# Layer 0 attention emitted by a phase in a group's period, and layer 1's row transforms stored frequency by frequency

## The chip, the core and the metric

The kernel runs on one core of one Trainium2 chip. The core has a matrix engine (TensorE, called PE in the profile; its weight loads are listed apart as PEld), a vector engine (VectorE, DVE), a scalar engine (ScalarE, ACT), a general engine (GpSimd, POOL) and SyncE (SP), which here only issues transfers. Each engine works through its own queue strictly in order; an instruction at the head of a queue waits until what it reads is written and what it overwrites has been read. Data lies in SBUF (128 partitions) and in PSUM, the accumulators into which PE writes.

The metric is the device time of one execution in microseconds. The kernel before takes 3742.2 us, the median of three runs (3740.39 to 3743.42). The profile comes from a further execution of the same program.

## The reference

The input `x` has 4 batches of 32 time steps, each 128 nodes by 128 features, in fp32 (8 MB). It goes through three layers in two sublayers each. The change touches layer 0 and the start of layer 1; the rest is an attention with a linear kernel and an expert network (layer 2), and a linear attention and a recurrent network (layer 3). Cut to what matters here:

```python
# layer 0:  x = x + conv_attn_hybrid(group_norm(x, 32 groups))
def gat(h, adj):                    # 128 images of 128 nodes x 128 features, 4 heads of 32
    q, k, v = heads(h @ Wq), heads(h @ Wk), heads(h @ Wv)
    scores = einsum('bnhd,bmhd->bhnm', q, k) / sqrt(32)
    scores = where(adj == 0, -1e9, scores)
    return h + softmax(scores) @ v @ Wo + bo
def mamba(xt):                      # every node a sequence of 32 steps, 256 channels, 16 states
    xc, z = split(xt @ in_proj); xc = silu(conv4(xc) + conv_b)
    dbc = xc @ x_proj               # 8 numbers for dt, B (16), C (16)
    dt = softplus(dbc[..., :8] @ dt_w + dt_b)
    h_t = exp(dt_t * A) * h_{t-1} + (dt_t * xc_t) * B_t        # the scan
    y_t = sum_s(h_t * C_t) + Dp * xc_t
    return (y * silu(z)) @ out_w + out_b
h  = layernorm(h + gat(h))          # per image
xt = layernorm(xt + mamba(xt))      # per node, after a transposition

# layer 1:  every 128 x 128 image is a token: instance norm, spectral convolutions for
#           keys, queries, values (rfft2, 16 x 9 modes), attention over 32 tokens, two mixers
x_ft = rfftn(instance_norm(tokens)) # the rows' transform: 65 numbers (cos, sin) of 128 columns
```

## The kernel before, in words

**Layer 0** runs batch by batch (four batches, b0 to b3), and each batch has two stages: the attention (`gat`) and the scan (`mamba`). All of `x` lies in SBUF in the tile `X`.

*The attention stage* treats a batch as eight groups of four time steps, so a tile is 128 x 512. For one group, in the order of the data: PE transposes the four images of `X` (kind `x`), DVE normalises them (`hg`, L454), PE forms q and k (`q`, L458), ACT copies them out (`qo`, L461), PE forms the values (`v`, L467) and DVE copies them (`vo`, L470). PE writes the scores of the four heads with the mask added (`sc`, L538 and L546). For each head DVE takes the row minima (`smin`, L555; the scores carry a minus sign), ACT exponentiates (`expo`, four instructions each, L560), DVE sums and inverts (`den`, L567 and L568), POOL scales (`scale`, L572). For each of the four images PE transposes the scaled weights (`turn`, L273), DVE or ACT copies them (`eT`, L580) and PE multiplies by the values (`att`, L587). ACT fetches the attention output (`o`, L594), PE projects it (`proj`, L600), DVE adds the residual (`r`, L604), which POOL made before (`base`, L531), and takes the statistics (`stats`, L609, L611); POOL raises the variance to the power -1/2 (`power`, L615 to L618), ACT normalises (`norm`, L623), PE transposes back and ACT stores the result to `h1` (`store`, L632).

Four more pieces of work lie in the same stage. (1) The end of the batch before, its output's normalisation (kinds `csums`, `cstats`, `cpower`, `cnorm`, L966 to L1010). (2) The group-norm statistics of the next batch (`gat_head`, one kind `head`): eight transposes of `X` each followed by a DVE statistic (L368), then DVE L377, PE L382, DVE L386 to L389, PE L382, DVE L392, and POOL's power L395. (3) The opening of the next batch (`gat_open`, kind `diag`): DVE L411 to L416, which read what L395 wrote, PE L420 and ACT L424. (4) The preparation of the first four scan steps (`mamba_block`): the convolution on PE (`conv`, eight products of 0.87 us, L1105), SiLU on ACT (L1112), the product for dt, B and C (L1117) and its copy `dbc` (L1121), the dt projection (L1128), and then softplus as a chain: ACT `abs` (L1136), ACT `exp` (L1139), DVE `relu` (L1144), ACT `one` (L1150), ACT `ln` (L1153), ACT `back` (L1156), POOL `dplus` (L1159), POOL `dsub` (L1162); last DVE `umul` (L1173), which the first states of the scan read. ACT holds one function table at a time; a change between SiLU, exp and ln is an instruction of 1.28 us in the trace.

*The scan stage* takes 32 steps of 16 states. In each step, four times: POOL multiplies dt by A (the decay, L822, tile `e` with three buffers), ACT exponentiates (L828), DVE multiplies by the state (L842) and adds the input (L850, four instructions, or one, L862, with the inputs made on ACT, L858); PE reads the state out (L880) with diagonal matrices that ACT (L834) and POOL (L839, tile `Dp`) make. The first step's states are made on ACT without a decay (L852).

*What sets the order.* Each stage is written as parts: (engine, estimated cost, function, predecessors, buffers taken and freed). `Parts.emit` sorts them into one sequence. With `by_rank` it takes, again and again, the part of lowest rank among those whose predecessors and buffers have been emitted; `mamba` uses it already, the rank being step group x period + a phase per kind. Without it, it plans: it keeps an estimated clock per engine, looks at the first `window` parts, takes the earliest start and within `patience` of it the lowest rank, and counts 1.3 us for a change of ACT's table. `gat` uses the planner, with a rank of `at * 144.5 + GAT_RANKS[kind]` and `PREP_RANKS` for the preparation. `in_order` then fixes this sequence as each engine's queue. So the ranks decide what stands ahead of what on PE, DVE, ACT and POOL; SP's queue and the DMAs have no part in it, since a batch's `X` is loaded once at the start (the loads of batches 1 to 3 are issued then too).

**Layer 1** opens with `images`. PE transforms the rows of each image by the matrix `fr` (`rows`, L1442), four images a round, 32 rounds; ACT copies the 4 x 65 results into `Fr` (`rows_out`, L1445) and squares the image (L1449), DVE sums the squares (`groups`, L1453), PE sums those over the rows (`total`, L1457). Products without use (`stir`, L1437) stand between them. `Fr` is a view [128, image t, frequency k] of a flat tile. Then come the norm's statistics (from the frequency 0, L1483), a scaling of `Fr` in eight pieces on DVE (L1540), POOL's rewrite of frequency 0 (L1549, L1550), the products `pr` of `Fr` with `rw` (L1565 to L1567) with ACT's copies (L1568), and the column transforms `px` (L1581 to L1588): here `Fr` for one frequency, 128 rows x 128 images, is the stationary operand of PE, 32 such products and four idle ones, ended by DVE's copies (L1590). 32 products `pG` of a copy `Rb` with itself follow (L1597).

## Time and profile before

| What | Value |
|---|---|
| Median of three runs | 3742.2 us (3740.39 to 3743.42) |
| Profiled execution, its own time | 3746.08 us |
| Its span in the profile | 3744.2 us |
| Mean granted PE clock | 0.90 |
| Busy share PE, DVE, ACT, POOL | 85%, 77%, 70%, 66% |
| First row minimum to last attention output, b0 to b3 | 36.6 to 147.7, 588.9 to 695.5, 1134.8 to 1244.4, 1684.0 to 1792.7 us |
| First scan decay to last, b0 to b3 | 158.7 to 571.8, 707.1 to 1118.6, 1254.5 to 1667.5, 1802.7 to 2211.5 us |
| `px` products of layer 1 | 2309.3 to 2325.6 us |
| `pG` products of layer 1 | 2325.6 to 2334.3 us |

The profile is of one execution of 3746.08 us; its span, from the first instruction to the last, is 3744.2 us. Times of single instructions are microseconds from the span's start. The busy shares are means over the whole program; the stages have different limits, so a stage is read from its own stretch. In the slices of the page each digit is the busy share of a fortieth of the span (93.6 us) in tenths, and the line PEclk is the clock that PE was granted in tenths of full speed. A group's line gives engine, operation, output and input with shapes, the number, the busy time and the mean of one, and after the bar the time its engine had been idle before these instructions, with what ended most of it.

### The profile page before, as it was taken

To read this page: it belongs to the slowest core of one execution; us is meant where nothing else is said; L and a number is where in the kernel's file an instruction comes from. 1 tells how busy PE (TensorE), PEld (TensorE's weight loads), DVE (VectorE), ACT (ScalarE), POOL (GpSimd) and SP (SyncE) were. 2 spreads that over 40 slices of the span, in tenths; PEclk is the share of its full clock that TensorE was granted. 3 is DMA by queue.
4 is the path that set the end of the run, shared out by engine and by line. 5 is a ranking of instruction groups with operands and counts; after the bars stand their busy time and mean duration, and the time that the engine had idled before them with its cause. 6 is when DMAs were issued, how large, how long until landed. Compare 5 with 4: busy or idle time off the path is not lost.

```text
span 3744.2 us, 64945 instructions
## 1 busy us (share of the span) xinstructions
PE 3178.7 (85%) x23839; PEld 2061.9 (55%) x23839; DVE 2888.3 (77%) x6980; ACT 2619.5 (70%) x5560; POOL 2454.3 (66%) x1985
## 2 busy tenths in 40 slices
PE   7799988799888799988799988788868977898878
PEld 4455555455555455555455557555547744587655
DVE  6699997699997799987699975778869756386942
ACT  5788886798886898877889863344556664175753
POOL 3689996699996699986799960333456432076940
PEclk8899989899999899989899988888769998998999
DMA  3000000000000000000000000000020001600003
GB/s 129 1 1 1 1 1 1 1 1 1 1 1 1 1 1 1 1 1 1 1 1 1 1 20 1 1 1 1 1 91 10 1 1 47 231 1 1 1 1 91
DMA packets 51656, 61.41 MB, mean 16 GB/s; under 512 B 5850, under 2 KB 31140, under 8 KB 51204
## 3 DMA queue, kind: packets, MB, share of 16 engines
q1 hardware_dynamic: 36740, 42.12, 3.3%
q10 hardware_dynamic: 14592, 15.08, 1.2%
q8 instruction: 190, 3.11, 0.3%
q14 instruction: 134, 1.10, 0.1%
HBM read 48.80 MB, written 8.39 MB: 15 GB/s over the span
## 4 chain that ended last, share of the span: by engine, by line
PE 19%; DVE 19%; ACT 6%; POOL 3%; issue 3%; DMA 2%; SPq 0%; DVEq 0%; ACTq 0%; POOLq 0%
DVE S L850 3%; DVE pa L842 3%; PE pc L1905 2%; PE pc L1868 1%; PE pb L1883 1%; PE pt L273 1%; PE pr L3242 1%; PE pr L3235 1%; DMA w<-in_L_ffn_weight_dram 1%; PE kv L2946 1%; DVE xn L2303 1%; DVE S L862 1%; DVE t L2160 1%; PE pc L3085 1%; PE pc L1922 1%
## 5 line engine op out<-in xcount | busy, mean ns | idle before, releaser
L822 POOL TENSOR_TENSOR e<-dt,Ar 128x1024 f32<-128x1024 f32 x496 | 1190.3, 2429 | 38.4 <-ACT pa L828 36.2
L842 DVE TENSOR_TENSOR pa<-pa,S 128x1024 f32<-128x1024 f32 x496 | 608.3, 1226 | 100.9 <-ACT pa L828 100.0
L850 DVE SCALAR_TENSOR_TENSOR S<-u,BC,pa 128x256 f32<-128x256 f32 x1488 | 611.7, 476 | 22.8 <-PE yp L880 10.8
L828 ACT ACTIVATE pa<-e 128x1024 f32<-128x1024 f32 x496 | 505.2, 1019 | 135.2 <-POOL e L822 73.9
L880 PE MATMUL yp<-S,Dp 64*64 64x256 f32 x4096 | 344.5, 475 | 2.6 <-ACT S L852 1.6
L880 PE MATMUL yp<-S,D 64*64 64x256 f32 x4096 | 300.5, 407 | 42.7 <-DVE S L850 19.5
L880 PEld LDWEIGHTS yp<-S,D 64*64 64x64 f32 x4096 | 178.3, 145 | 172.4 <-DVE S L850 48.4
L834 ACT ACTIVATE D<-I,BC 128x64 f32<-128x64 f32 x1024 | 263.4, 336 | 0.1
L880 PEld LDWEIGHTS yp<-S,Dp 64*64 64x64 f32 x4096 | 169.5, 163 | 157.0 <-issue 68.6
L1105 PE MATMUL pm<-h,Wm 128*128 128x512 f32 x512 | 255.2, 620 | 0.0
L572 POOL TENSOR_TENSOR e<-e,den 128x512 f32<-128x512 f32 x128 | 131.4, 1039 | 122.2 <-DVE den L568 69.9
L858 ACT ACTIVATE ub<-u,BC 128x256 f32<-128x256 f32 x496 | 210.3, 495 | 0.3 <-DVE S L862 0.3
L898 PE MATMUL pm<-I,y 128*128 128x64 f32 x1024 | 150.3, 270 | 39.9 <-ACT y L888 39.9
L560 ACT ACTIVATE e<-sc,mn 128x128 f32<-128x128 f32 x512 | 145.2, 396 | 30.8 <-DVE mn L555 24.3
L898 PEld LDWEIGHTS pm<-I,y 128*128 128x128 f32 x1024 | 137.2, 194 | 49.1 <-ACT y L888 48.6
L839 POOL TENSOR_TENSOR Dp<-I,BC 128x256 f32<-128x256 f32 x256 | 157.2, 629 | 7.3 <-issue 7.3
L862 DVE TENSOR_TENSOR S<-pa,ub 128x1024 f32<-128x1024 f32 x124 | 151.1, 1219 | 4.1 <-ACT ub L858 0.2
L1105 PEld LDWEIGHTS pm<-h,Wm 128*128 128x128 f32 x512 | 88.0, 192 | 97.8 <-issue 80.7
L869 PE MATMUL yp<-Wm,ident 128*128 128x256 f32 x256 | 100.1, 478 | 48.8 <-ACT y L888 37.8
L555 DVE TENSOR_REDUCE mn<-sc 128x4 f32<-128x512 f32 x128 | 83.1, 681 | 58.7 <-PE sc L546 41.3
L893 PE MATMUL pm<-xc,DD 128*128 128x128 f32 x512 | 115.5, 307 | 4.4 <-DVE v L470 2.8
L1159 POOL TENSOR_TENSOR dt<-dt,u 128x1024 f32<-128x1024 f32 x32 | 75.5, 2360 | 59.0 <-ACT u L1153 59.0
(612 smaller groups left out, 8074.0 us busy)
## 6 DMA issues: line engine op xcount, KB each, us to landing
w<-in_L_ffn_weight_dram SPq DMA_DIRECT2D x22, 1024.0 KB, 14.9
w<-in_L_ffn_weight_dram ACTq DMA_DIRECT2D x10, 1024.0 KB, 14.2
out_dram<-o ACTq DMA_DIRECT2D x16, 256.0 KB, 2.9
out_dram<-o SPq DMA_DIRECT2D x16, 256.0 KB, 2.9
X<-in_x_dram SPq DMA_DIRECT2D x4, 512.0 KB, 4.8
A<-in_L_conv_A_log_dram SPq DMA_DIRECT2D x1, 2048.0 KB
cw<-in_L_conv_conv_w_dram SPq DMA_DIRECT2D x1, 512.0 KB
sh<-in_sh_dram SPq DMA_DIRECT2D x1, 512.0 KB
```

Of the source, the lines that this page charges most:

```text
L560: nc.scalar.activation(e[:, i, :], v["sc", h // 2][:, h % 2, i * P : (i + 1) * P], AF.Exp, scale=-1.0, bias=v["mn"][:, 4 * h + i : 4 * h + ...
L822: nc.gpsimd.tensor_tensor(v["e", q], node("dt").unsqueeze(1).to_broadcast([P, 4, 256]), Ar[:, 4 * q : 4 * q + 4, :], ALU.mult)
L828: nc.scalar.activation(v["a", q], v.pop(("e", q)), AF.Exp, scale=-1.0)
L834: nc.scalar.activation(v["D", q][:, r, :], I2, AF.Copy, scale=g["BC"][:, i, s : s + 1])
L839: nc.gpsimd.tensor_tensor(v["D", q], I2.unsqueeze(1).to_broadcast([P, 4, 64]), C, ALU.mult)
L842: nc.vector.tensor_tensor(v["a", q], v["a", q], S[:, 4 * q : 4 * q + 4, :], ALU.mult)
L850: nc.vector.scalar_tensor_tensor(S[:, s, :], node("u"), Bt, a[:, r, :], ALU.mult, ALU.add)
L858: nc.scalar.activation(v["b", q][:, r, :], node("u"), AF.Copy, scale=g["BC"][:, i, s : s + 1])
L862: nc.vector.tensor_tensor(S4, v.pop(("a", q)), v.pop(("b", q)), ALU.add)
L880: nc.tensor.matmul(v["y"][o : o + 64, n, :256], D[ns, r, :], S[ns, s, :], start=(s < 2), stop=(s >= 14), skip_group_check=True,)
L898: nc.tensor.matmul(v["p"][:, o : o + 64], v["y"][:, n, j * P : (j + 1) * P], I2, start=False, stop=(n == 1))
L1105: nc.tensor.matmul(g["x", j], Wm[:, q, j * P : (j + 1) * P], rows(4 * k + 3 - q), start=(q == 0), stop=(q == 3))
```

## The change

In layer 0, `gat` no longer plans. It sets `by_rank`, and a part's rank is the group's number times `GAT_PERIOD` plus a phase from `GAT_PHASES`, one per instance of a kind within a group (four for the four heads, 22 for the next batch's statistics). The closing parts of the batch before, the next batch's statistics and the preparation of the scan get phases of the same scale (kinds beginning with `c`, `head`, kinds beginning with `p`). The parts themselves, their predecessors and their buffers stay. The costs of the parts and `STRETCH` are edited beside them (one example is shown); the planner alone reads them, and this stage no longer uses it.

In layer 1, `Fr` becomes a view [128, frequency k, image t]: the rows' copies write transposed, the scaling, POOL's rewrite and the `pr` products take the other order, ACT's copies of `pr` run straight, and the stationary operand of a `px` product is 128 numbers side by side in place of 128 numbers 65 apart. In round 2 ten products without use of 512 columns stand ahead of `total`, where four stood behind it.

```diff
@@ -328,27 +328,68 @@
         return Wq, Wk, Wv, Wo, g4, far, identb, bo, nsg, nsb
 
 
-    GAT_RANKS = dict(
-        att=-3667.5, back=260, base=-11401, cnorm=19461, cpower=16969.5, cstats=-14046, csums=-2469,
-        den=-4706.5, diag=13731, eT=-6150, expo=17585, head=3158.5, hg=1067, norm=13992.5, o=-3580,
-        power=1837.5, proj=-256, q=-975, qo=-11362.5, r=1709, sc=-2224.5, scale=15762.5, smin=2891, stats=3672,
-        store=-1872.5, turn=-8022.5, v=16866, vo=-13144.5, x=-1207.5,
+    GAT_PERIOD = 13.873
+
+    GAT_PHASES = dict(
+        att=(43.17, 47.23, 51.52, 55.84),
+        back=(91.39,),
+        base=(44.71, 45.1),
+        cnorm=(-152.35,),
+        cpower=(-179.88,),
+        cstats=(-110.36,),
+        csums=(-439.61, -162.69, 141.8),
+        den=(-154.28, 33.13, -147.2, 38.09),
+        diag=(0, 0, 0, 0,
...
+        eT=(42.85, 45.28, 49.62, -132.38),
+        expo=(-129.7, 30.87, 35.85, 34.64),
+        head=(-86.83, -15.71, 29.14, -112.82, 29.32, -151.41, 45, -219.78, 126.27, -346.88, 153.77, 103.91,
+            163.07, 199.51, 173.07, 393.09, 178.51, -114.71, 218.17, 164.3, 226.97, 211.01),
+        hg=(11.65,),
+        norm=(65.37,),
+        o=(56.82,),
+        pback=(173.32,),
+        pbc=(-101.27,),
+        pbct=(160.53,),
+        pconv=(135.08, 135.08, -135.33, 6.91, 139.7, 143.45, 182.88, 251.31),
+        pdabs=(114.96, 160.52),
+        pdbc=(263.56,),
+        pdexp=(168.41, 373.45),
+        pdln=(159.59,),
+        pdplus=(172.32,),
+        pdsub=(208.08,),
+        pdtproj=(113.5, -52.72),
+        pone=(-22.14,),
+        power=(60.13,),
+        prelu=(172.01, 380.2),
+        proj=(56.9,),
+        pumul=(412.11, 456.88),
+        pxproj=(148.65,),
+        pxsilu=(-288.93, 144.55),
+        pxturn=(606.06, 420.33),
+        q=(-174.72, 14.25),
+        qo=(14.55, 16.05),
+        r=(-123.4,),
+        sc=(23.77,),
+        scale=(40.38, -149.71, -146.96, 41.09),
+        smin=(25.93, -154.82, -154.42, -156.43),
+        stats=(58.04,),
+        store=(92.77,),
+        turn=(42.58, -136.88, 48.51, -129.57),
+        v=(32.79,),
+        vo=(38.07,),
+        x=(9.51,),
     )
 
-    PREP_RANKS = dict(
-        back=6847, bc=-3164.5, bct=4342.5, conv=1651, dabs=-4328, dbc=-1187, dexp=3646.5, dln=5483,
-        dplus=-11118, dsub=-22178, dtproj=1225.5, one=6330, relu=-4091.5, umul=-8012, xproj=2450, xsilu=3831,
-        xturn=-11453,
-    )
-
     def gat_head(self, plan, b, gw, c, pm, after=()):
 
         nc, X, PE, DVE, ACT, POOL = self.nc, self.X, "PE", "DVE", "ACT", "POOL"
-        g4, hold, v, last = gw[4], plan.hold, {}, []
+        g4, hold, v, last, seen = gw[4], plan.hold, {}, [], {}
         d = [None]
 
         def add(*args):
-            plan.rank = self.GAT_RANKS["head"]
+            n = seen["head"] = seen.get("head", -1) + 1
+            plan.rank = self.GAT_PHASES["head"][n]
             return plan.add(*args)
 
         def bank():
     def gat(self, b, early, h1, S, d, gw, mw, w, m, w2, ew, ps, po, px, pm):
-        plan = Parts(latency=0.25, window=250, patience=0.15, stretch=Parts.STRETCH)
-        hold, pace = plan.hold, 144.5
-
-        def add(kind, at, *args, **kwargs):
-            plan.rank = at * pace + self.GAT_RANKS[kind]
+        plan, seen = Parts(), {}
+        plan.by_rank, hold = True, plan.hold
+
+        def add(kind, g, *args, **kwargs):
+            n = seen[kind, g] = seen.get((kind, g), -1) + 1
+            plan.rank = g * self.GAT_PERIOD + self.GAT_PHASES[kind][n]
             return plan.add(*args, **kwargs)
 
...
-            s.pop("close")(lambda kind, at, *args, **kwargs: add("c" + kind, 0, *args, **kwargs))
+            s.pop("close")(lambda kind, k, *args, **kwargs: add("c" + kind, 0, *args, **kwargs))
...
-                mins.append(add("smin", g + i / 8, DVE, 0.62, lambda i=i: smin(i), [sc, *mins], () if i else [h["mn"]]))
+                mins.append(add("smin", g, DVE, 0.6, lambda i=i: smin(i), [sc, *mins], () if i else [h["mn"]]))
...
-        def prepare(kind, at, *args, **kwargs):
-            plan.rank = self.PREP_RANKS[kind]
-            return plan.add(*args, **kwargs)
+        def prepare(kind, k, *args, **kwargs):
+            return add("p" + kind, 0, *args, **kwargs)
 
...
@@ -1415,7 +1456,7 @@
...
         flat = XG.rearrange("p a b -> p (a b)")
-        Fr = flat[:, : BT * 65].rearrange("p (t k) -> p t k", k=65)
+        Fr = flat[:, : BT * 65].rearrange("p (k t) -> p k t", k=65)
...
@@ -1442,7 +1483,7 @@
                     nc.tensor.matmul(p[:, i, :], X[:, 4 * u + i, :], self.fr, start=True, stop=True)
 
             def rows_out(u):
-                nc.scalar.copy(Fr[:, unit(u), :], S[u].pop("p"))
+                nc.scalar.copy(Fr[:, :, unit(u)], S[u].pop("p").rearrange("p t k -> p k t"))
 
...
@@ -1460,10 +1501,10 @@
                 for r in range(U + 2):
                     run(rows, r)
                     stir(128)
+                    if r == 2:
+                        for _ in range(10):
+                            stir(512)
                     run(total, r - 2)
-                    if r == 2:
-                        for _ in range(4):
-                            stir(512)
...
@@ -1476,7 +1517,7 @@
 
 
         with self.pool("l1ps", 2, True) as ps:
-            F0 = Fr[:, :, 0].rearrange("p (b t) -> p b t", b=B)
+            F0 = Fr[:, 0, :].rearrange("p (b t) -> p b t", b=B)
...
@@ -1538,16 +1579,16 @@
             for q in range(8):
                 ts = slice(16 * q, 16 * q + 16)
                 nc.vector.scalar_tensor_tensor(
-                    Fr[:, ts, 1:],
-                    Fr[:, ts, 1:],
+                    Fr[:, 1:, ts],
+                    Fr[:, 1:, ts],
                     rs[:, 0, q // 2 : q // 2 + 1],
-                    sr[:, 0, ts].unsqueeze(2).to_broadcast([P, 16, 64]),
+                    sr[:, 0, ts].unsqueeze(1).to_broadcast([P, 64, 16]),
                     ALU.mult,
                     ALU.mult,
                 )
                 if q == 0:
                     nc.gpsimd.tensor_tensor(vf, vf, sr[:, 0, :], ALU.mult)
-                    nc.gpsimd.tensor_tensor(Fr[:, :, 0], vf, sr[:, 1, :], ALU.add)
+                    nc.gpsimd.tensor_tensor(Fr[:, 0, :], vf, sr[:, 1, :], ALU.add)
 
...
@@ -1561,11 +1602,11 @@
             Rb = flat[:, BT * 65 : BT * 65 + 32 * P].rearrange("p (k t) -> p k t", t=P)
             for q in range(8):
                 ts = slice(16 * q, 16 * q + 16)
-                p = pr.tile([P, 16, 32], F32, tag="pr", name="pr")
-                nc.tensor.matmul(p[:64], rw[:, :64], Fr[:, ts, 0:32], start=True, stop=True)
-                nc.tensor.matmul(p[64:], rw[:, :64], Fr[:, ts, 32:64], start=True, stop=False)
-                nc.tensor.matmul(p[64:, :, 0], rw[:, 64:], Fr[:, ts, 64], start=False, stop=True)
-                nc.scalar.copy(Rb[:, :, ts], p.rearrange("p t k -> p k t"))
+                p = pr.tile([P, 32, 16], F32, tag="pr", name="pr")
+                nc.tensor.matmul(p[:64], rw[:, :64], Fr[:, 0:32, ts], start=True, stop=True)
+                nc.tensor.matmul(p[64:], rw[:, :64], Fr[:, 32:64, ts], start=True, stop=False)
+                nc.tensor.matmul(p[64:, 0, :], rw[:, 64:], Fr[:, 64, ts], start=False, stop=True)
+                nc.scalar.copy(Rb[:, :, ts], p)
...
@@ -1578,14 +1619,14 @@
                 lo = p[:, 2 if k in (0, 15, 16) else (k - 1) // 7, : 14 * 34].rearrange("p (n c) -> p n c", c=34)
                 if k in (0, 16):
                     o = lo[:, 3 if k == 0 else 1, :]
-                    nc.tensor.matmul(o, Fr[:, :, k], fw[:, 0, :], start=True, stop=k == 0)
+                    nc.tensor.matmul(o, Fr[:, k, :], fw[:, 0, :], start=True, stop=k == 0)
                     if k:
-                        nc.tensor.matmul(o, Fr[:, :, 32 + k], fw[:, 2, :], start=False, stop=True)
+                        nc.tensor.matmul(o, Fr[:, 32 + k, :], fw[:, 2, :], start=False, stop=True)
                     continue
                 j = (k - 1) % 7
                 o = lo[:, 0:3:2, :] if k == 15 else lo[:, j : 14 - j : 13 - 2 * j, :]
-                nc.tensor.matmul(o, Fr[:, :, k], fw[:, 0:1, :].to_broadcast([P, 2, 34]), start=True, stop=False)
-                nc.tensor.matmul(o, Fr[:, :, 32 + k], fw[:, 1:3, :], start=False, stop=True)
+                nc.tensor.matmul(o, Fr[:, k, :], fw[:, 0:1, :].to_broadcast([P, 2, 34]), start=True, stop=False)
+                nc.tensor.matmul(o, Fr[:, 32 + k, :], fw[:, 1:3, :], start=False, stop=True)
```

## The prediction

> **What bounds the kernel now.** The change touches two places, so I read the page for their share, then each stretch on its own. First the page: the span, and the slices of PE, DVE, ACT and POOL with PE's granted clock.
>
> ```profile
> span 3744.2 us, 64945 instructions
> PE   7799988799888799988799988788868977898878
> DVE  6699997699997799987699975778869756386942
> ACT  5788886798886898877889863344556664175753
> POOL 3689996699996699986799960333456432076940
> PEclk8899989899999899989899988888769998998999
> ```
>
> The span repeats one pattern four times up to slice 24: an attention stage of about 1.4 slices in which DVE and POOL drop to 6 or 7, then a scan at 9. That is layer 0, a batch at a time. Its attention stages, from first row minimum to last attention output, are the next view: busy time of PE, PEld, DVE, ACT, POOL, then granted clock, of batches 1, 0, 2, 3.
>
> ```profile
> 588.90:695.50 106.60, 90.55 (x852) 55.51 (x850) 77.76 (x194) 81.16 (x213) 64.93 (x80) 0.98 0.01 1
> 36.60:147.70 111.10, 94.96 (x858) 58.14 (x859) 79.10 (x194) 80.17 (x210) 59.66 (x73) 0.94 0.04 16
> 1134.80:1244.40 109.60, 93.86 (x857) 57.34 (x856) 78.53 (x195) 81.41 (x213) 65.03 (x80) 0.95 0.01 1
> 1684.00:1792.70 108.70, 90.34 (x842) 54.72 (x840) 76.32 (x191) 81.29 (x213) 65.00 (x80) 0.95 0.00 1
> ```
>
> No engine is full: PE 85%, the others 60 to 76%. The stage is bound by chains between the engines' queues, which is what an order can change. DVE's groups over batch 1's stage (number | busy, mean ns | idle before):
>
> ```profile
> L567 DVE TENSOR_REDUCE den<-e 128x4 f32<-128x512 f32 x32 | 21.6, 674 | 1.7 <-ACT e L560 1.2
> L555 DVE TENSOR_REDUCE mn<-sc 128x4 f32<-128x512 f32 x32 | 20.8, 680 | 11.2 <-PE sc L546 8.8 <-ACT e L560 2.4
> L580 DVE COPY eT<-pm 128x512 f32<-128x512 f32 x16 | 10.9, 679 | 5.7 <-PE pm L273 5.7
> ```
>
> The second place is layer 1's row transforms. In order of time (start, us, what), with a pair of each kind of weight load and two lines for a clash of DVE with POOL that I need below:
>
> ```profile
> 712.33 2.39 POOL L822 TENSOR_TENSOR e<-dt,Ar 128x1024 f32<-128x1024 f32 x1
> 712.43 2.31 DVE L411 TENSOR_TENSOR gc<-gd 128x1 f32<-128x1 f32 x1 [6.22 <-POOL gd L395]
> ...
> 2310.36 0.56 PEld L1587 LDWEIGHTS px<-fw,XG 128*128 128x128 f32 x2
> 2310.82 0.56 PEld L1588 LDWEIGHTS px<-fw,XG 128*128 128x128 f32 x2
> ...
> 2325.63 8.71 PEld L1597 LDWEIGHTS pG<-XG 128*128 128x128 f32 x64
> 2325.97 1.61 DVE L1590 COPY Xm<-px 128x238 f32<-128x238 f32 x6 [20.14 <-PE px L1583]
> ...
> 2583.65 5.47 POOL L2080 TENSOR_TENSOR X<-X,t 128x256 f32<-128x256 f32 x8
> 2583.68 5.52 DVE L1982 TENSOR_TENSOR dg<-n,ident 16x64 f32<-16x64 f32 x1
> ```
>
> The px products step by 0.46 us a pair at full clock, their weights being a column of `Fr` at a stride of 65 numbers; the pG products, whose weights lie side by side, step by 0.22 once the clock is full. DVE waits 20.1 us for px: PE alone sets this stretch.
>
> **Layer 1, part by part.** *Weights in line.* From 2309.26 to 2325.63 (16.4 us) PE does 32 px pairs and 4 filler pairs. At 0.235 a pair (between pG's 0.22 and the row transforms' 0.97 us for four pairs) that is 36 x 0.235 = 8.5: -7.9. Ends: 0 if the stride isn't the reason; -0.9 if the clock stands at half throughout (pairs of in-line weights step by 0.43 at 2284 to 2286, half clock). I take -7.9, since pG is the nearest row. *pG after it* starts at half clock (until 2328.8) and takes 8.7; 32 pairs at 0.22 are 7.1: -1.5, or 0. *Gaps in POOL's write*: L1550 writes `Fr`'s first frequency with a stride in 1.32 us, its twin L1549 in line in 0.45; PE waits for it at 2297.6, so -0.8. *Ten idle products ahead of `total`, for four behind it.* PE waits 4.1 us for `sg` from 2228.4; the ten fill that. A product costs 0.86 at full clock (two of the 0.43 us instructions of L1437): 8.6 us to 2237.0 against 2237.8 before, -0.8. If the half-clock step of 2229.8 to 2236.6 still comes they end at 2240.4, +2.6; all at half +7.7. Between these I take 0. *Copies that now transpose* (L1445, runs of four numbers, PSUM read at a stride): L1264 writes such runs and reads PSUM at a stride, 578 ns for 512, as a straight copy of 512 takes; so 357 stays 357, and up to 0.35 more a copy is covered by ACT's wait for DVE in each 1.34 us round (16.8 us in 32). Upper end +0.1 a round, +3. *Scaling L1540* in runs of 16: 1.27 each, 0, upper end +2; the rw products likewise 0. Sum: -7.9 - 1.5 - 0.8 = -10.
>
> A rule of the Trainium skill (SBUF — State Buffer, "Door 1: The DMA port swizzle") speaks both ways here: SBUF serves 16-byte lines, so strided fp32 reads pay, while any PSUM access out of line slows matmuls. The first half agrees with 0.46 against 0.22. The second says nothing of ACT's reads; the L1264 row shows none slowed.
>
> **Layer 0, the steady groups.** The order of the built program now repeats one pattern on each engine. A group's DVE work is 4 x 0.65 (mn) + 4 x (0.674 + 0.178) (den) + 2 x 0.68 (eT) + 0.68 (r) + 0.86 + 0.36 (statistics) + 0.80 (hg) + 0.68 (v) = 10.75 us. Following PE, ACT and POOL along it by the rows' durations, only `eT` after the fourth product waits, by about 0.15: 10.9 a group. Before, groups stand 8.9, 9.4, 11.3, 11.5, 15.0, 12.3 and 10.8 apart (batch 1), 79.3 in all, 83.7, 82.2 and 81.4 in batches 0, 2, 3. After: 9.6 for the first (the last block's normalisation now precedes the first exponentials, which start 3.0 us later: power 1.8 and norm 1.65 less the overlap), 5 x 10.9, and 10.1 without hg: 74.2. Savings 9.5, 5.1, 8.0, 7.2. Bounds for a step: 10.75, and the 11.4 of the least disturbed steps before. Lost at the start: 0.8 in batches 1 and 2 (one head statistic ahead of the first minimum), 2.2 in batch 0, where PE's first instruction reads batch 1's x, which lands at 30.6 us.
>
> *Last minimum to last attention output.* 27.3 before. PE has eight convolution products (0.87 each) in one run there instead of spread, but no dt projection: by the rows 24.5 (23.5 in batch 3, no head). -2.8 x 3 - 3.8. So the last output `o` comes 10.1, 7.1, 10.0 and 11.0 us earlier: 38.
>
> *From there to the scan.* The whole dt chain now stands behind `o` on ACT: dbc and the first dt product until 2.1, abs 0.55, table 1.28, exp 0.55, abs 0.5, exp 0.55, one 1.1, table 1.28, ln 1.05, so 9.0; store, norm, back to 12.3. On POOL dplus 9.1 to 11.4, three Dp (they wait for norm) to 13.1, dsub to 15.5. Before, dsub ended 4.4 us after `o`, since this chain ran under the last group. Then DVE: umul, which the scan's first states S need, is now queued behind L411 to L416, which wait for POOL's power L395, itself behind dsub, and for L387 to L389, which meet dplus, Dp and dsub on POOL and run only at 15.5: power ends at 17.5. Three decays (7.1 together, as at 1802.7) follow without a gap. L411 starts under them; in L1982's row DVE sat through eight POOL instructions in a row, so I let it wait to 24.6; umul 26.0; eight S, D, four S, table and one exp on ACT 8.5; first update L850 at 35.7. Before it stands at +26.5, +26.5, +25.6 and +20.6. In batch 3, without head, it is +30.7. Loss 9.2 + 9.2 + 10.1 + 10.1 = 38.6. Lower end: L411 passes at once (as its 159 ns in batch 0's start), 7 less a batch; upper: nothing further.
>
> By the Trainium skill (SBUF — State Buffer, "SBUF: two separate sides") the loser of the shared DVE and POOL port blocks for the other's whole instruction. Read so, L411 waits for one decay, 2.4, and the sum would be 4.7 x 3 = 14 lower. The row of L1982 (5.52 us under eight) says the whole run; it decides.
>
> So layer 0 is -38 + 38.6, about -1 with the table loads left out (8 fewer in the order, 1.28 each, on ACT where it waits anyway). Scan and later stages keep their order.
>
> **Sum**: -10 - 1 = -11, from the profiled execution's 3746.1 to 3735; that execution lies 3.9 above the median of 3742.2, so 3731. Runs differ by 0.1%; under 0.2% (7.5 us) I call no change.
>
> **Rivals.**
> - *The scan isn't held.* L411 slips in after the first decay (7.1 less 2.4 a batch, 14 over three), or the steps reach the floor 10.75: -14 and -3 more, 3714. For: POOL's `e` tile has three buffers, so its run ends; against: L1982's row.
> - *The clock turns it (slower).* With normalisation ahead of the exponentials PE has some 9 us with 3 us of work at each stage's start. In layer 1 a gap of 4.1 us stands beside a 6.8 us step at half clock (0.67 in that 10 us). One such step in the first groups costs PE 3.4 us of work, two 6.8; PE leads every group's chain. At 5 a batch: +20 - 11 = +9, 3751; it decides from 4.6 a batch. Against: 0.98 in batch 1 now, with a similar gap at 590.
> - *The weights don't gain.* If the px pairs run at half clock, layer 1 gives 2 and groups stay at 11.4: 3742 less 1, no change. Against: the clock was full from 2301 to 2315 even with slower loads.
>
> **How the numbers follow.** Forecast 0.38, own range 3723 to 3738; scan not held 0.26; clock 0.18; no gain 0.18. Faster: 0.3 + 0.26 + 0.04 = 0.6; same 0.08 + 0.13 = 0.21; slower 0.19. The range takes in the second case with both its savings and some of the tail's, down to 3706, and the clock case up to 3752.
>
> **What will show it.** Right: px pairs at 0.22 to 0.24 and L1590's wait near 12; minima of successive groups 10.8 to 11.0 apart; L411 with 7 us beside three decays; L850 35 us after the last `o`. Wrong if groups stand 11.4 or more apart, if the half clock shows at a stage's start, or if umul is not behind L411 in time.

## The result

The change made the kernel slower, by 0.4%: 3755.8 us (median of five runs, 3753.7 to 3762.5) against 3740.6 (five runs, 3737.9 to 3743.4). The ratio is 1.0042, with a 95% interval of 1.0028 to 1.0057. The forecast was 3731 with a range of 3706 to 3752 and 0.6 on faster. It missed in sign, and the measured median lies 4 us above the range.

The profiled execution of the changed kernel took 3755.1 us, its span is 3753.3. In its source the lines of `gat` stand 42 lower than before and those of the opening, the scan and layer 1 stand 41 lower, so L555 is now L597, L411 is L452, L850 is L891 and L1590 is L1631. First the page's slices of the changed kernel (span, then PE, DVE, ACT, POOL and PE's granted clock):

```profile
span 3753.3 us, 64973 instructions
PE   6799988798888798888799988788868987998887
DVE  6699998699998699997599986778879756386942
ACT  4789886798986788886788873444556654176753
POOL 3599996699995699996699980333456432077940
PEclk8899989899999898999899888888769998998989
```

The picture at this scale is the same as before. The loss is in the borders of stages. The same view as in the prediction, the attention stages from first row minimum to last attention output (busy time of PE, PEld, DVE, ACT, POOL, then granted clock), of batches 1, 0, 2, 3 of the changed kernel:

```profile
596.10:697.10 101.00, 88.58 (x848) 54.66 (x846) 78.17 (x192) 71.20 (x205) 68.59 (x81) 0.98 0.01 1
43.60:144.60 101.00, 90.84 (x868) 56.37 (x868) 79.67 (x194) 70.69 (x203) 63.76 (x76) 1.00 0.01 1
1148.30:1249.80 101.50, 89.01 (x848) 55.10 (x847) 78.37 (x192) 71.27 (x205) 68.62 (x81) 0.97 0.01 2
1702.90:1804.70 101.80, 86.69 (x826) 52.61 (x824) 76.42 (x189) 71.24 (x204) 69.14 (x83) 0.97 0.01 1
```

All four stages are shorter (101 to 102 us, against 107 to 111). The order shortened its stages. What it gives there is taken back between the last attention output and the scan. This is DVE's queue at that border of batch 1, in order of time (start, duration, line; in brackets the idle time before). The last attention output ended at 697.1:

```profile
710.93 2.27 DVE L430 TENSOR_TENSOR gd<-gd,gmv 128x1 f32<-128x1 f32 x1
713.93 0.16 DVE L433 TENSOR_SCALAR gd<-pm 128x1 f32<-128x1 f32 x1 [0.74 <-PE pm L423]
714.76 2.36 DVE L452 TENSOR_TENSOR gc<-gd 128x1 f32<-128x1 f32 x1 [0.67 <-POOL gd L436]
717.16 2.26 DVE L453 SCALAR_TENSOR_TENSOR gc<-gd,gc 128x1 f32<-128x1 f32 x1
719.46 2.26 DVE L454 TENSOR_TENSOR gc<-gc,bo 128x1 f32<-128x1 f32 x1
721.64 0.27 DVE L457 TENSOR_SCALAR hg<-ident,gc 128x128 f32<-128x128 f32 x1
721.84 1.27 DVE L1214 TENSOR_TENSOR u<-dt,pm 128x512 f32<-128x512 f32 x2
723.03 0.28 DVE L457 TENSOR_SCALAR hg<-ident,gc 128x128 f32<-128x128 f32 x1
730.77 1.23 DVE L883 TENSOR_TENSOR pa<-pa,S 128x1024 f32<-128x1024 f32 x1 [7.46 <-ACT pa L869]
732.11 1.66 DVE L891 SCALAR_TENSOR_TENSOR S<-u,BC,pa 128x256 f32<-128x256 f32 x4
```

And POOL's decays beside it:

```profile
714.70 7.00 POOL L863 TENSOR_TENSOR e<-dt,Ar 128x1024 f32<-128x1024 f32 x3
```

Three instructions on 128 numbers each (L452, L453, L454) take 6.9 us together, beside three decays that run for 7.0 us. `umul` (L1214), from which the first states of the scan are made, stands behind them. The first multiplication by the state (L883) comes 33.6 us after the attention output. Before, it came at 22.1 in this batch (the output ended at 695.5), and of the three instructions only the first, L411, met a decay; the other two ran while POOL stood idle:

```profile
714.77 0.16 DVE L412 SCALAR_TENSOR_TENSOR gc<-gd,gc 128x1 f32<-128x1 f32 x1
714.97 0.16 DVE L413 TENSOR_TENSOR gc<-gc,bo 128x1 f32<-128x1 f32 x1
717.61 1.22 DVE L842 TENSOR_TENSOR pa<-pa,S 128x1024 f32<-128x1024 f32 x1
721.99 1.66 DVE L850 SCALAR_TENSOR_TENSOR S<-u,BC,pa 128x256 f32<-128x256 f32 x4 [3.17 <-PE yp L880]
```

From the two profiles, where the time went, in us (each row is a difference of marks in the changed kernel's trace and the same marks before):

| Stretch | b0 | b1 | b2 | b3 | Sum |
|---|---|---|---|---|---|
| End of the scan before (b0: start) to first row minimum | +7.0 | +0.1 | +1.1 | -0.2 | +8.0 |
| First row minimum to last attention output | -10.0 | -5.5 | -8.1 | -7.0 | -30.7 |
| Last attention output to the last decay of the scan | +10.1 | +10.8 | +13.8 | +12.8 | +47.5 |
| Layer 0 | | | | | +24.8 |
| Last decay to the end of `pG` in layer 1 | | | | | -10.2 |
| End of `pG` to the end | | | | | -5.4 |

The sum is 9.2; the spans differ by 9.1. The medians differ by 15.1, because the profiled execution before was 5.5 us over its later median.

Layer 1 gained what was forecast. These are loads of `px`'s stationary operand in the changed kernel (two instructions each line) and the copy that waits for them:

```profile
2334.07 0.30 PEld L1628 LDWEIGHTS px<-fw,XG 128*128 128x128 f32 x2
2334.30 0.30 PEld L1629 LDWEIGHTS px<-fw,XG 128*128 128x128 f32 x2
2341.97 1.61 DVE L1631 COPY Xm<-px 128x238 f32<-128x238 f32 x6 [11.65 <-PE px L1624]
```

A pair now steps by 0.22 to 0.23 us, not 0.46, and DVE waits 11.65 us, not 20.1.

### The profile page after: what moved, and what is told of

Same layout as the page of the kernel before. It is cut to its first block, busy times and chain, and to the rows that moved or that the text cites. A ratio compares the mean times of both kernels' runs of the same rounds, so it can differ in the third digit from the quotient of the medians.

```text
span 3753.3 us, 64973 instructions
## 1 busy us (share of the span) xinstructions
PE 3169.6 (84%) x23851; PEld 2054.4 (55%) x23851; DVE 2904.4 (77%) x6980; ACT 2606.0 (69%) x5552; POOL 2451.5 (65%) x1985
## 5 line engine op out<-in xcount | busy, mean ns | idle before, releaser
L883 DVE TENSOR_TENSOR pa<-pa,S 128x1024 f32<-128x1024 f32 x496 | 609.1, 1228 | 122.8 <-ACT pa L869 122.3
L891 DVE SCALAR_TENSOR_TENSOR S<-u,BC,pa 128x256 f32<-128x256 f32 x1488 | 612.0, 478 | 12.8 <-DVE pa L883 0.5
L939 PE MATMUL pm<-I,y 128*128 128x64 f32 x1024 | 153.7, 274 | 43.6 <-ACT y L929 43.6
L2951 ACT ACTIVATE xn<-X,xnb,xrs 128x128 f32<-128x128 f32 x192 | 80.7, 487 | 41.8 <-DMA lnw<-in_L_attn_ln_w_dram 30.2
## 6 DMA issues: line engine op xcount, KB each, us to landing
w<-in_L_ffn_weight_dram ACTq DMA_DIRECT2D x10, 1024.0 KB, 14.6
```

The lines of the kernel that those rows point to most:

```text
L883: nc.vector.tensor_tensor(v["a", q], v["a", q], S[:, 4 * q : 4 * q + 4, :], ALU.mult)
L891: nc.vector.scalar_tensor_tensor(S[:, s, :], node("u"), Bt, a[:, r, :], ALU.mult, ALU.add)
L939: nc.tensor.matmul(v["p"][:, o : o + 64], v["y"][:, n, j * P : (j + 1) * P], I2, start=False, stop=(n == 1))
```

## The experiments

Theory after the result: the layer 1 part gives its 10 us, the attention order costs 25, and this cost sits at three places. DVE's small instructions that wait for decays hold `umul` (batches 0 to 2). In batch 3 ACT's softplus chain stands behind the last normalisation. In batch 0 PE waits for a transfer at the start. The rivals are that the parts don't add up, that a start of the scan is held by something else in the chain, or that the place in a queue costs whatever stands there.

All medians, with the kernel before measured beside them on the same chip:

| Kernel | Median us | Before us | Ratio (95%) |
|---|---|---|---|
| the change | 3755.8 | 3740.6 | 1.0042 (1.0028 to 1.0057) |
| l1_only | 3731.5 | 3738.5 | 0.9981 (0.9972 to 0.9990) |
| l0_only | 3766.0 | 3738.5 | 1.0073 (1.0059 to 1.0086) |
| umul_first | 3738.5 | 3738.5 | 1.0001 (0.9991 to 1.0011) |
| dbc_ahead | 3750.4 | 3738.5 | 1.0033 (1.0021 to 1.0045) |
| pool_open | 3731.0 | 3741.2 | 0.9971 (0.9962 to 0.9979) |
| head_late | 3750.1 | 3741.2 | 1.0023 (1.0014 to 1.0033) |
| all_three | 3721.7 | 3741.2 | 0.9950 (0.9936 to 0.9964) |
| layout_only | 3726.6 | 3741.2 | 0.9963 (0.9949 to 0.9977) |
| best | 3722.8 | 3741.9 | 0.9958 (0.9944 to 0.9971) |
| conv_behind | 3787.0 | 3741.9 | 1.0128 (1.0113 to 1.0144) |
| layout_again | 3735.9 | 3741.9 | 0.9986 (0.9977 to 0.9995) |
| one_input | 3734.0 | 3741.5 | 0.9982 (0.9973 to 0.9991) |

Below, a time "under the changed kernel" is a difference to its 3755.8. The changed kernel was measured in the first round alone, and the kernel before, measured anew beside each round, lay between 3738.5 and 3741.9. So such differences are good to some 3 us, and where they are of that size the traces carry the argument.

### The two halves by themselves

`l1_only` is the kernel before with the `images` function of the change; `l0_only` is the changed kernel with the `images` function of before. Their edits are the two halves of the diff above.

> The kernel before with the layer 1 part alone (the layout of Fr by frequency and the ten idle products), layer 0 as before. The profile of the change shows 8.0 us less from the first px product to the last, 1.4 less for pG and 0.7 less ahead of them, 10.2 together, and another 5.4 us less spread over stages behind, whose code is the same. Theory A: only the 10.2 belong to the change, so 3740.6 - 10 = 3730.6. Theory B: the 5.4 behind belong to it too (it moves where the clock's steps fall), so 3725. Theory C: the gain at px is given back later, 3740.

> The changed kernel with layer 1 as before, so the order of the attention stage alone. By the profile of the change the last decay of batch 3 ends 24.8 us later than before. Theory A: layer 0's order costs 25 and the parts add up, so 3740.6 + 25 = 3766, 10 over the changed kernel's 3755.8. Rival: the order costs 15 and layer 1 gave nothing, 3756.

Measured: 3731.5 and 3766.0. The halves add up within the intervals (-7.0 and +27.4 against the kernel beside them, +20.4 together; the whole change +15.1, with an interval of 10 to 21). The attention order is what made the kernel slower, and layer 1 is a gain. Theory B of `l1_only`, which adds the 5.4 us of the stages behind, stays open. In its own trace the stretch from the end of `pG` to the end takes 1404.4 us, but in `dbc_ahead`, which has the same layer 1, 1409.2. The two traces with the old layer 1 took 1409.6 (before) and 1408.4 (`l0_only`); the twelve with the new layout lie between 1402.3 and 1409.4. The median of `l1_only`, 7.0 under the kernel beside it, is nearer to theory A's 10 than to 15.

### umul ahead of the opening

`in_order` fixes each engine's order within one block of the program. Here the scan's block goes on, for DVE, from the last instruction of the attention's block. `umul` is written in the attention's block and the next batch's opening in the scan's, so the opening can't stand ahead of `umul`.

```diff
-    def in_order(self):
+    def in_order(self, join=None):
...
-        last = {}
+        last = dict(join or {})
...
-                last[e] = ins.name
+                last[e] = ins.name; self.ends = last
...
-        with self.in_order():
+        with self.in_order({mybir.EngineType.DVE: self.ends[mybir.EngineType.DVE]}):
             plan.emit()
```

> The changed kernel with one swap on DVE in batches 0 to 2: the two umul stand ahead of the opening of the next batch (the lines of L411 to L416 of before). Theory A: the scan starts late because umul waits behind three small instructions that each sit through a decay of POOL. umul then ends 18 to 19 us after the last attention output, not 26.0, the first states and the first exponential follow, and the first multiplication by the state comes at about 27, not 33.6: 6.8 a batch, three batches, -20, so 3736; the three small instructions stay at 2.3 each. Rival: the scan's start hangs on dsub, which ends 16 us after the output, and on the opening, which still ends at 24.7 ahead of the first multiplication; then less than 2 a batch, 3750 to 3756.

Measured: 3738.5, 17 us under the changed kernel (expected 20). DVE's queue of batch 1 in this kernel, in order of time; the last attention output ended at 695.5:

```profile
713.74 1.47 DVE L1214 TENSOR_TENSOR u<-dt,pm 128x512 f32<-128x512 f32 x2 [1.28 <-PE pm L1211]
715.13 0.33 DVE L452 TENSOR_TENSOR gc<-gd 128x1 f32<-128x1 f32 x1
715.50 2.30 DVE L453 SCALAR_TENSOR_TENSOR gc<-gd,gc 128x1 f32<-128x1 f32 x1
717.83 2.31 DVE L454 TENSOR_TENSOR gc<-gc,bo 128x1 f32<-128x1 f32 x1
720.06 0.47 DVE L457 TENSOR_SCALAR hg<-ident,gc 128x128 f32<-128x128 f32 x2
722.68 1.23 DVE L883 TENSOR_TENSOR pa<-pa,S 128x1024 f32<-128x1024 f32 x1 [2.15 <-ACT pa L869]
```

Two of the small instructions still wait for a decay each, but `umul` no longer stands behind them. The first multiplication comes 27.2 us after the output in batches 0 to 2, not 33.6. The rival, that the start hangs on `dsub` and the opening whatever the order, falls: `dsub` still ends at 16.0.

### The same order, with the three instructions on POOL

```diff
-            nc.vector.tensor_tensor(c[:, 0:1], d[0][:, 2:3], d[0][:, 2:3], ALU.add)
-            nc.vector.scalar_tensor_tensor(c[:, 1:2], d[0][:, 0:1], -1.0, c[:, 0:1], ALU.mult, ALU.mult)
-            nc.vector.tensor_tensor(c[:, 1:2], c[:, 1:2], bo, ALU.add)
+            nc.gpsimd.tensor_tensor(c[:, 0:1], d[0][:, 2:3], d[0][:, 2:3], ALU.add)
+            nc.gpsimd.tensor_scalar(c[:, 1:2], d[0][:, 0:1], -1.0, None, ALU.mult); nc.gpsimd.tensor_tensor(c[:, 1:2], c[:, 1:2], c[:, 0:1], ALU.mult)
+            nc.gpsimd.tensor_tensor(c[:, 1:2], c[:, 1:2], bo, ALU.add)
```

> The changed kernel with the order of DVE kept (umul behind the opening of the next batch), but the three small instructions that read what POOL's power wrote are made on POOL itself, behind the power and ahead of the decays (four instructions of about 0.2 us). Theory A: not the place behind the power costs, but that each of the three waited for a decay (2.36, 2.26, 2.26 us). The remaining opening then ends about 19 us after the last attention output, umul at 20 to 20.5, and the first multiplication by the state comes at 28 to 29 (33.6 in the changed kernel): 5 a batch, -15, so 3741. Rival: the place in the queue is what costs, whatever engine makes the three: the time stays at 3756 within 3, or rises by the 0.8 that the decays start later, 3758.

Measured: 3731.0, 25 us under the changed kernel, more than the 15 expected. `umul` still stands behind the opening, and ends 18.7 us after the output, since the three now take 0.19 to 0.24 each on POOL ahead of the decays. The first multiplication comes at 26.4, where I had said 28 to 29. One reason for the difference is in the trace: the `Dp` products, which stood between `dplus` and `dsub` in the changed kernel, moved behind the opening in this build, so `dsub` ended at 15.4 and the small instructions L428 to L430 took 0.16 each; in the changed kernel L430 sat through `dsub` for 2.27. The rival, that the place in the queue is what costs, falls.

### The same order and engine, with one tensor input each

```diff
-            nc.vector.tensor_tensor(c[:, 0:1], d[0][:, 2:3], d[0][:, 2:3], ALU.add)
-            nc.vector.scalar_tensor_tensor(c[:, 1:2], d[0][:, 0:1], -1.0, c[:, 0:1], ALU.mult, ALU.mult)
-            nc.vector.tensor_tensor(c[:, 1:2], c[:, 1:2], bo, ALU.add)
+            nc.vector.tensor_scalar(c[:, 0:1], d[0][:, 2:3], 2.0, None, ALU.mult)
+            nc.vector.tensor_scalar(c[:, 1:2], d[0][:, 0:1], -1.0, c[:, 0:1], ALU.mult, ALU.mult)
+            nc.vector.tensor_scalar(c[:, 1:2], c[:, 1:2], bo, None, ALU.add)
```

> The changed kernel with the three small instructions of the opening still on DVE and still ahead of umul, but each written with one tensor input and its other operand as a scalar per row (two were tensor by tensor, one read two tensors). In the trace of the changed kernel the forms with two inputs from SBUF took 2.26 to 2.36 us beside decays, while the update of X's normalised input (one input, from PSUM) took 0.78 to 0.81 beside decays as elsewhere. Theory A: the form is what waits, so each takes 0.15 to 0.2, umul ends at 19 to 20 after the last attention output and the first multiplication by the state comes at 27, not 33.6: 6.6 a batch in three batches, so 3736. Theory B: any DVE instruction that reads SBUF waits for a decay: 2.3 each again and 3756. The Trainium skill (SBUF — State Buffer, "SBUF: two separate sides") says that only a DVE instruction in a two-port mode or with two inputs from SBUF takes the pair that it shares with GpSimd; that is Theory A's side.

Measured: 3734.0, 22 us under the changed kernel. DVE and POOL of batch 1 in this kernel, in order of time (the attention output ended at 690.6):

```profile
708.15 0.15 DVE L452 TENSOR_SCALAR gc<-gd 128x1 f32<-128x1 f32 x1 [0.67 <-POOL gd L436]
708.34 0.21 DVE L453 TENSOR_SCALAR gc<-gd,gc 128x1 f32<-128x1 f32 x1
708.59 0.21 DVE L454 TENSOR_SCALAR gc<-gc,bo 128x1 f32<-128x1 f32 x1
708.76 1.47 DVE L1214 TENSOR_TENSOR u<-dt,pm 128x512 f32<-128x512 f32 x2
710.14 2.81 DVE L457 TENSOR_SCALAR hg<-ident,gc 128x128 f32<-128x128 f32 x2
717.70 1.23 DVE L883 TENSOR_TENSOR pa<-pa,S 128x1024 f32<-128x1024 f32 x1 [4.75 <-ACT pa L869]
```

```profile
708.08 7.16 POOL L863 TENSOR_TENSOR e<-dt,Ar 128x1024 f32<-128x1024 f32 x3
```

The same three results, in the same place of the same queue, beside the same decays, take 0.15 to 0.21 us instead of 2.26 to 2.36. So the form of the instruction is what waits. That is the cause of 6.4 us a batch in batches 0 to 2 (27.2 us to the first multiplication, not 33.6). The rest of the loss at this border is not tested by itself: 27.2 is still 5 to 7 us later than before (20.6 to 22.1), and `dsub` ends 16.0 us after the output where it ended at 4.4, since the softplus chain now stands behind that output. The rule of the Trainium skill (SBUF — State Buffer, "SBUF: two separate sides") that a DVE instruction takes the pair shared with GpSimd only in a two-port mode or with two inputs from SBUF, and then blocks for the other's whole instruction, agrees here: two inputs 2.3 us, one input on 128 numbers 0.2 us, and `umul`, whose second input lies in PSUM, 0.7 each. L457, one input of 128 x 128 fp32 from SBUF, waited once (2.81 for the two, 0.55 at rest); the page's two-port mode would cover that, and no run here tests it alone. A wait for two decays, which the rule as the page puts it does not give, shows in `all_three` (last section).

### The chain of batch 3

```diff
-        pdbc=(263.56,),
+        pdbc=(155,),
```

> The changed kernel with one phase changed (pdbc 263.56 to 155): in batch 3 alone ACT's dbc and the softplus chain then stand ahead of the last normalisation, as they do in batches 0 to 2. Theory A: in batch 3 the wait of that normalisation for POOL's statistics (2.8 us, and 1.65 of work) holds the whole chain; dsub then ends 16 us after the last output, not 22.1, and the time falls by 5.5 to 3750. Rival: the chain is not what starts batch 3's scan (store and norm only move behind it): under 1.

Measured: 3750.4, 5.4 under the changed kernel. ACT's queue of batch 3 in the changed kernel (the output is the copy of L636):

```profile
1804.09 0.58 ACT L636 COPY o<-po 128x512 f32<-128x512 f32 x1 [0.60 <-PE po L629]
1806.36 0.78 ACT L674 ACTIVATE h<-pm,nsb,nsg 128x512 f32<-128x512 f32 x1 [1.69 <-PE pm L273]
1809.91 1.65 ACT L665 ACTIVATE S<-r,lnb,lrs 128x128 f32<-128x128 f32 x4 [2.78 <-POOL lnb L660]
1811.46 0.67 ACT L1162 ACTIVATE dbc<-pm,ident 41x512 f32<-41x512 f32 x1
```

and with the one phase changed:

```profile
1800.95 0.59 ACT L636 COPY o<-po 128x512 f32<-128x512 f32 x1 [0.60 <-PE po L629]
1801.43 0.68 ACT L1162 ACTIVATE dbc<-pm,ident 41x512 f32<-41x512 f32 x1
1803.84 0.60 ACT L1177 ACTIVATE u<-pm 128x512 f32<-128x512 f32 x1 [1.72 <-PE pm L1169]
```

`dbc` comes right behind the output, `dsub` ends 16.1 us after it, not 22.1, and the first multiplication by the state at 25.0, not 31.0.

### The start of batch 0

```diff
-        head=(-86.83, -15.71, ...
+        head=(24, -15.71, ...
```

> The changed kernel with one phase changed (the first of head, -86.83 to 24): the first transposition of the next batch's input stands behind the first scores on PE, and in batch 0 no longer ahead of everything. Theory A: in batch 0 PE sat from 17.8 to 30.6 us for that input's transfer; the first row minimum then comes at 36.6 as before, not 43.6, and the time falls by 6 to 7 to 3749. In batches 1 and 2 nothing (0.6 either way). Rival: the first minimum waits for other setup work (the half-clock step, the filter weights, ACT's Ar) and stays above 41: under 2.

Measured: 3750.1, 5.6 under the changed kernel. PE's queue at the start of the changed kernel:

```profile
17.46 0.35 PE L423 MATMUL pm<-gd,g 128*128 128x1 f32 x2 [0.93 <-DVE gd L430]
30.63 1.11 PE L273 MATMUL pm<-ident,X 128*128 128x128 f32 x4 [12.82 <-DMA X<-in_x_dram]
```

and the first row minimum with the transposition placed later:

```profile
34.11 2.48 DVE L597 TENSOR_REDUCE mn<-sc 128x4 f32<-128x512 f32 x4 [1.28 <-ACT Ar L761]
```

In the changed kernel PE's first attention instruction read the next batch's `X` and waited 12.8 us for it, with the whole first group behind it. With the phase moved, the first minimum comes at 34.1 (43.6 in the changed kernel); the groups behind give 2.2 us of that back (103.2 to the last output, not 101.0).

### The last group

```diff
-        pconv=(135.08, 135.08, -135.33, 6.91, 139.7, 143.45, 182.88, 251.31),
+        pconv=(160, 160, 160, 160, 160, 160, 160, 160),
```

> The changed kernel with the eight convolution products of each batch's preparation behind the last group's attention products (the phases of pconv all 160). The forecast took 24.5 us from the last first-minimum to the last attention output, 25.9 were measured. Theory A: these eight products of 0.9 in PE's queue are what holds the last groups; without them it falls to 20 to 21, but the whole softplus chain then starts 7 later behind the output and dsub ends at o + 28, not 16. Net later by 7 in batches 0 to 2 and 2 in batch 3, so +20 to +24, 3776 to 3780. Rival: the last group is held by its own chain of exponentials, sums and scalings; then the output comes no earlier and the time is +30 or more.

Measured: 3787.0, 31 us over the changed kernel, and neither theory fits alone. From the last group's first minimum to the last output it takes 21.5 to 22.3 us, not 25.6 to 25.9, so the eight convolution products hold 3.6 to 4.1 us of it, less than the 5 to 6 I expected. `dsub` ends 27.0 to 29.6 us after the output. What remains without them, most of the last group's time, I read as its own chain: in batch 1 of this kernel PE's transpositions wait 0.45 for POOL's scaling and its attention products 1.78 for ACT's copy. The trade is real, and the changed kernel stands on its better side.

### Layer 1's layout without the idle products

```diff
-                    if r == 2:
-                        for _ in range(10):
-                            stir(512)
                     run(total, r - 2)
+                    if r == 2:
+                        for _ in range(4):
+                            stir(512)
```

(on the kernel `l1_only`)

> The kernel before with the layout of Fr by frequency, but the idle products as before (four behind total). Theory A: px and pG gain 9.4 by the loads of weights in line alone, and the ten idle products are worth the 0 that I took (ends -0.8 and +2.6): from the last decay to the end of pG 113 to 114 us, against 123 before and 112 to 113 with them; the time within 2 of layer 1's part alone, 3731.5. Rival: the idle products hold the clock up through the rows and give several us: then 116 or more and 3735.

> The kernel before with the layout of Fr by frequency alone, once more, beside the two others. Theory A: 10 to 11 us from the stage of px and pG, so 3727 to 3731 and 7 to 11 over the mended kernel. Theory B: the 14.6 of the first time hold again (the stages behind gain too), 3726 or under.

Measured: 3726.6 and, with the same kernel on another chip, 3735.9; the ratios are 0.9963 (0.9949 to 0.9977) and 0.9986 (0.9977 to 0.9995). From the last decay to the end of `pG` the two took 112.2 and 113.1 us, `l1_only` with the ten idle products 111.4, the kernel before 123.0. So the idle products are worth about nothing, within 2 us; the layout gives 10 to 12 us in its stage. Theory B, that 14.6 hold, falls: the second time it is 6.0, which is also a little under the 7 to 11 of theory A. What moves the whole time by several more us lies behind: the unchanged stretch from the end of `pG` to the end took 1402.3 and 1409.4 us in these two. That spread was seen in kernels of all kinds here and I have no cause for it.

### The repairs together

`all_three` joins `umul_first`, `dbc_ahead` and `head_late`; `best` joins `pool_open`, `dbc_ahead`, `head_late` and the idle products of before.

> The changed kernel with the three repairs together: umul first, dbc ahead in batch 3, the first head transposition late. Theory A: the three lie on separate stretches of one chain and add up: 3755.8 - 17 - 5.4 - 6.5 = 3727, which is 11 under the kernel before and 4 under layer 1's part alone (3731.5): the order of the groups is then worth a little. Rival: the repairs overlap (the later stages fill what one of them frees), 3733 or more.

> The changed kernel with the three small instructions of the opening on POOL, dbc ahead in batch 3, the first head transposition late, and the idle products of layer 1 as in the kernel before (four behind total). Theory A: the gains add: 3731 (the three on POOL) - 5.4 - 5.7 = 3720, the idle products 0; about 20 under the kernel before and 7 to 11 under layer 1's layout alone, which is what the order of the groups is worth once the scan's start is mended. Rival: the start of the scan is then held by the softplus chain alone in all batches, the groups' gain is used up, and it comes out level with layer 1's layout alone.

Measured: 3721.7 and 3722.8, against 3741.2 and 3741.9: ratios 0.9950 and 0.9958, so both are faster than both kernels. The repairs add up within some 6 us (34 and 33 us under the changed kernel, where their sums are 17 + 5.4 + 5.6 = 28 and, with POOL in place of `umul`, 36). The attention stages of `all_three`, in the view shown above:

```profile
34.60:136.30 101.70, 90.42 (x864) 57.50 (x864) 79.74 (x194) 70.69 (x203) 63.78 (x76) 0.98 0.06 22
581.50:682.60 101.10, 88.41 (x844) 54.50 (x844) 78.35 (x193) 71.19 (x205) 68.67 (x81) 0.97 0.01 1
1127.70:1228.80 101.10, 88.42 (x844) 54.50 (x844) 78.28 (x193) 71.25 (x205) 68.53 (x81) 0.97 0.01 2
1673.30:1775.10 101.80, 87.41 (x826) 52.91 (x824) 76.40 (x189) 71.38 (x205) 69.14 (x83) 0.95 0.00 1
```

The groups are as short as in the changed kernel, and the start of the scan no longer eats it. Beside `best`, the layout alone took 3735.9, 13 us more; beside `all_three` it took 3726.6, 5 us more. In the traces the last decay of layer 0 ends at 2199.7 and 2200.2 in these two, at 2206.2 to 2211.5 in the four kernels with the old order. So the order of the groups is worth 5 to 13 us once its borders are mended.

## Why the prediction was wrong, step by step

- **Layer 1, right: -10 forecast, -10.2 measured.** The 32 `px` pairs and their four idle ones took 8.4 us (8.5 forecast, 16.4 before), `pG` 1.5 less (1.5 forecast), the idle products nothing (0). That the strided loads hold a pair at 0.46 us is in the trace of before: it stepped so both at full clock and in the half-clock step from 2315.1. But the whole gain needs the full clock too, as in-line pairs at half clock stepped by 0.43 in that trace. The granted clock over `px` was 0.68 in the two traces with the old layout and 1.00 in all twelve with the new one; why it stayed full is not shown. One term was wrong in kind: POOL's write L1550 was to lose 0.8 with its gaps, and took 1.31 us, 1.32 before; so the stride was not what it paid for, and what it was is open. The stage up to `px` got shorter by 0.7 all the same.
- **The steady groups, right in size.** I said 10.9 us; the middle ones are 11.1 to 11.2. DVE does not wait 0.15 us a group but 0.8: 0.29 for the first `eT` in it, 0.29 for `r`, 0.22 for the second `eT`, as its queue between 626.6 and 637.8 shows. That and the first groups made the seven steps 75.1 to 76.2 where 74.2 was forecast: 5 us over four batches.
- **"By the rows 24.5", from last minimum to last attention output: too low.** 25.6 to 25.9 were measured, 6 us over four batches. I took 2.8 us off the 27.4 of before and 1.5 came (3.8 and 1.8 in batch 3). The run with the convolution behind shows what those eight products hold there, 3.6 to 4.1 us; which row of the working was too short is not shown.
- **The start of batch 0: +2.2 forecast, +7.0 measured.** I had seen that PE's first instruction reads the next batch's `X`, which lands at 30.6, and priced only part of the wait behind it: the granted clock was half when PE resumed (half from 18.0 to 41.9, where before it was half from 17.9 to 28.2; a projection of 1.0 us took 2.0), and the first row minimum came at 43.6.
- **"From there to the scan": the mechanism and the place were right, the sum was measured at the wrong mark.** I forecast that `umul` ends 26.0 us after the output; it ended at 26.0. I forecast the first update L850 at 35.7 (30.7 in batch 3), measured 35.0 (32.4), a loss of 38.2 where I said 38.6. But before, that first update waited 3.2 to 3.8 us for PE in batches 0 to 2, behind a multiplication that had already run, so part of its lateness was slack. At the update the loss of the four batches is 8.5, 8.5, 9.4 and 11.8; at the first multiplication it is 12.1, 11.6, 13.0 and 11.8, in sum 48.5; at the last decay, which counts, 10.1, 10.8, 13.8 and 12.8, in sum 47.5. So the sum of 38.2 at the update came near the forecast by luck: batches 0 to 2 lost less there than forecast, and batch 3 lost 1.7 more (32.4 against 30.7, for which the working shows no terms). This step is 9 us of the miss, 6 in batches 0 to 2 and 3 in batch 3.
- **L411's wait: right in sum, wrong in detail.** I let one instruction sit through three decays, by the row of L1982. In fact each of three waited for one decay (2.36, 2.26, 2.26). That the sum is the same is luck: three decays stood there, and three instructions. The skill's rule, which I set against that row, was the nearer one for a single instruction in this trace, and so was the row of L411 itself, 2.31 us beside one decay; I had not asked how many such instructions stand in a row.
- **The rivals.** "The scan isn't held" did not come: it is what `pool_open` and `one_input` then made. "The clock turns it" named the right sign and nearly the time (3751), but not the cause: in the stages the granted clock was 0.97 to 1.00, no lower than the 0.94 to 0.98 before; ahead of the first minimum it was 0.90 in batches 1 and 2, where it had been 1.00 and where 0.1 and 1.1 us were lost, and half in batch 0, behind the wait for `X`. "The weights don't gain" did not come: the pairs stepped by 0.22 at full clock. Its sum was off as well: steps of 11.4 in place of 10.9 are some 10 us over four batches by the forecast's own numbers, so 3749, not 3741.

In sum, the term that failed is layer 0, which was to be -1 and was +24.8. Its gain from the first minimum to the last output was put at 42 (9.5, 5.1, 8.0 and 7.2 for the groups, 12.2 for the last one) and was 30.7: 11 us. Its loss at the starts was put at 3.8 and was 8.0: 4 us. Its loss from the last output to the scan was put at 38.6 and was 47.5: 9 us. The last 1 is what I had given to the table loads without working it out, and no mark shows it. The forecast had a gain of 38 (the 42 less the starts) against a loss of 38.6, two large terms that nearly cancelled, and its range was too narrow for the errors of both.

## What to carry to other kernels

When an order is written anew, look at the border of the stage before its inside: a queue that feeds the next stage must not have a small instruction ahead of it that can wait. On DVE, beside a POOL that works without a gap, write a small instruction with one tensor input and a scalar per row, or move it to POOL: three instructions with two tensor inputs on 128 numbers cost 7 us here, three times over, and 0.6 in the other form. On 128 x 128 numbers the form with one tensor input did wait once (L457, above). And measure a loss at the mark that sets the pace after it, not at one that had slack before.

## What was not expected of the hardware

- In the changed kernel a DVE instruction with two inputs from SBUF waited for one decay of POOL (2.26 to 2.36 us beside decays of 2.33 to 2.41), and the next one again, so DVE got in at every border between two decays. It does not always: in `all_three` the same L453 sat through two decays, in each of batches 0 to 2. The rows of batch 1:

```profile
700.20 7.12 POOL L863 TENSOR_TENSOR e<-dt,Ar 128x1024 f32<-128x1024 f32 x3
702.66 4.68 DVE L453 SCALAR_TENSOR_TENSOR gc<-gd,gc 128x1 f32<-128x1 f32 x1
```

The row of 5.52 us under eight POOL instructions in the trace of before (L1982), in which DVE got in at none, may be of this kind. What decides how many it waits for stays open.
- ACT's copies that write transposed in runs of four numbers take 357 ns, as the straight ones did, and DVE's scaling in runs of 16 numbers takes 1.34 us in the mean, as before. Of the instructions that the new layout touches, only PE's loads of weights were seen to pay for the stride: two of them in 0.56 us at a stride of 65 numbers, 0.30 in line.
